# Moving Strassen's sums from GpSimd to VectorE, and the order of two kinds of additions in an attention loop

## The chip, the cores and the metric

The kernel runs on one core of a Trainium2 chip. The metric is the device time of one execution in microseconds (us); smaller is better. The engines are TensorE (PE in the profile; PEld is its weight load), VectorE (DVE), ScalarE (ACT), GpSimd (POOL), and SyncE (SP), whose queue issues most of the DMAs. Each engine executes its instructions in order and waits for the others through semaphores.

## The reference

A batch of 16 images of 256 channels and 32 x 32 pixels (1024 positions) goes through two layers, all in float32. Cut to what matters:

```python
# layer 0: attention over the 1024 positions, 4 heads of 64
qkv = xs @ w_proj + b_proj
attn = softmax(q @ k.T * 64 ** -0.5)
x = (attn @ v) @ w_out + b_out + xs
# layer 1: group norm, attention with 8 heads of 32, then an MLP of 256 -> 1024 -> 256
x = x + attention(group_norm(x), qkv_w, proj_w, proj_b, phys_bias)
h = gelu(mlp_w1 @ group_norm(x) + mlp_b1)
x = x + mlp_w2 @ h + mlp_b2
```

## The kernel before

Channels lie on the 128 partitions in two halves, positions on the free axis[...]. The images follow each other, and one image's stages are mixed with its neighbours' so that TensorE always has matmuls: `attention_a` (layer 0), the MLP's hidden layer of the image before, then `attention_b` (layer 1) with "filler" matmuls in it.

**The second attention** (`attention_b`) runs over 4 items (a position tile and a half of the heads) of 4 units, each unit two key blocks. A unit's `scores` (L502) write eight PSUM tiles, the first two into banks 0 and 1; ScalarE takes their exponentials into four tiles `e_b` of 128 x 1024 (L517, eight buffers). `weigh` multiplies the exponentials of the unit *before* with the values into bank 0 (L553), and the result is added to `res_b`: by ScalarE's copy for an item's first unit (L564), by VectorE for the others (L566). Only after that may the next unit's scores be written to bank 0. VectorE also sums the exponentials into two tiles `es_b` (L532), two additions for the first key block ("block 0") and two for the second. For an item's first unit only the second two exist. The order in the loop is: scores, the additions of block 0, the weighted sums of the unit before with their emptying of bank 0, the additions of block 1.

After a unit, `run` calls `later.tick()` (work put off by so many steps, such as the denominators) and then the unit's filler pieces. In the images 1 to 14 every unit has a filler: q, k and v of the layer 1 heads still missing, q, k and v of the next image's layer 0, and the output products of the previous image's MLP. In image 0 about half the units have none, in the last image (15) some.

**Denominators.** ScalarE copies the sums over keys (L328), SP moves them to a spread layout, VectorE inverts them (L337), SP writes and reads them back through DRAM (`row`, `rd_b`), and VectorE scales `res_b` (L600). GpSimd adds them up in `dsum` and `isum` (L339, L340).

**The MLP.** `hidden` computes 16 tiles `g` of 128 x 512 (matmul L849, Gelu on ScalarE L857). The output layer is a Strassen product: seven products of 128 x 128 blocks (`reduce`, matmul L314 with `m<-g,w2s`) instead of eight. Its right factors are sums and differences of g tiles, made in place by `combine` (L868), four instructions a call: two calls (differences) beside the hidden layer, one each after products 2, 3 and 4. Five of the seven products go to two output blocks: ScalarE copies the bank into a tile `lent` (L911, L914), and two instructions (L929) add or subtract it to the image's tile `x`. The other two go to one block, by one VectorE instruction from the bank (L925). A block that misses nothing more is stored by SP (L931). For all images but the last, L868 and L929 run on GpSimd; for the last, whose MLP stands alone at the end, on VectorE:

```python
add_to = nc.gpsimd if b < B - 1 else nc.vector
```

`nc.…` calls are given in the program's order; a scheduler then orders each engine's instructions by when it expects them to be ready, except those bound by `tc.keep_in_program_order`. The weights' Strassen sums (`sum_quarters`, at the start) stay on GpSimd in both kernels.

Of the kernel before, what the change touches and what calls it, by code (L numbers as in the profile page):

```python
# [11 lines left out]
ALU = mybir.AluOpType  # L12
AX = mybir.AxisListType

P = 128
# [4 lines left out]
TB = 512  # L20
# [215 lines left out]
def first_pass(ctx, tc, x, out, k):  # L236
    nc = tc.nc
    B, C, S = x.shape
    CC, SB, NT = C // P, S // P, S // TB
    HC = k["w1"].shape[2] // P  # L240
    later = Later()
# [25 lines left out]
    def wide(name, n=None):  # L267
        if n is None:
            n = next(m for m in order if m not in kept)
        use(n)  # L270
        return ps_s.tile([P, 2, TB], F32, tag=f"s{n}", name=name)
# [206 lines left out]
    def attention_b(b, qT, kT, v, project):  # L478
        key, D = f"b_{b}", D1
        G = P // D  # L480
# [5 lines left out]
        res, sums = {}, {}  # L486

        def scores(i, kb):
            t, c = items[i]
            es = []  # L490
            for m in range(2):
                if m == 0:
                    one, two = (bank(f"s_{key}_{i}_{kb}_{n}", n) for n in range(2))
                    tiles = [None, wide(f"s_{key}_{i}_{kb}_1")]
                    outs = [one, two, tiles[1][:, 0, :], tiles[1][:, 1, :]]
                else:
                    tiles = [wide(f"s_{key}_{i}_{kb + 1}_{n}") for n in range(2)]
                    outs = [tiles[g // 2][:, g % 2, :] for g in range(G)]
                for g in range(G):
                    for h in range(0, P, HALF):  # L500
                        k0 = (kb + m) * P + h
                        nc.tensor.matmul(  # L502
                            outs[g][h : h + HALF, :],
                            kT[g * D : (g + 1) * D, c, k0 : k0 + HALF],
                            qT[g * D : (g + 1) * D, c, t * TB : (t + 1) * TB],
                            start=True,
                            stop=True,
                        )
                for n in range(G // 2):
                    e = work.tile(  # L510
                        [P, 2, TB], F32, tag="e", name=f"e_{key}_{i}_{kb + m}_{n}", bufs=8
                    )
                    for to, s in (
                        [(e, tiles[n])] if tiles[n] is not None
                        else [(e[:, 0, :], one), (e[:, 1, :], two)]
                    ):
                        nc.scalar.activation(to, s, AF.Exp, scale=float(D) ** -0.5)  # L517
                    es.append(e)
            return i, kb, es

        def add(i, kb, es, block):
            if kb == 0 and block == 0:
                sums[i] = [
                    work.tile([P, 2, TB], F32, tag="es", name=f"es_{key}_{i}_{n}", bufs=4)
                    for n in range(G // 2)
                ]
                return
            for n in range(G // 2):  # L530
                d = sums[i][n]
                ins = nc.vector.tensor_add(d, es[n] if kb == 0 else d, es[2 * block + n])  # L532
                if block:
                    tc.keep_in_program_order(ins)


# [72 lines left out]
        pending = None  # L609
        for u in units:  # L610
            now = scores(*u)
            add(*now, 0)
            if not pending:

                yield
                add(*now, 1)
                pending = now
                continue
            weigh(*pending)
            add(*now, 1)  # L620
            pending = now
            yield
        weigh(*pending)
# [217 lines left out]
    def mlp(b, xb, hn):  # L841
        n4 = HC // 2
        gs = {}
        add_to = nc.gpsimd if b < B - 1 else nc.vector

        def hidden(t, hc):
            ps = wide(f"m1_{b}_{t}_{hc}")[:, 0, :]
            for cc in range(CC):
                nc.tensor.matmul(  # L849
                    ps,  # L850
                    k["w1"][:, cc, hc * P : (hc + 1) * P],
                    hn[0][:, cc, t * TB : (t + 1) * TB],
                    start=(cc == 0),
                    stop=(cc == CC - 1),
                )
            g = work.tile([P, TB], F32, tag="g", name=f"g_{b}_{t}_{hc}", bufs=16)
            nc.scalar.activation(g, ps, AF.Gelu, bias=k["m1b"][:, hc : hc + 1])  # L857
            gs[hc // n4, t, hc % n4] = g
            if (t, hc) == (1, n4):
                combine((1, 0), (0, 0), False)  # L860
            if (t, hc) == (1, HC - 1):
                combine((0, 1), (1, 1), False)


        def combine(to, what, plus):
            for i in range(n4):
                d = gs[(*to, i)]
                ins = (add_to.tensor_add if plus else add_to.tensor_sub)(  # L868
                    d, d, gs[(*what, i)]
                )  # L870
                tc.keep_in_program_order(ins)

        products = [
# [7 lines left out]
        ]  # L883
        missing = {(0, 0): 4, (0, 1): 2, (1, 0): 2, (1, 1): 4}
        lent = []

        def reduce(number, right, outs, then):
            ps = wide(f"m2_{b}_{number}")[:, 0, :]  # L890
            for i in range(n4):
                product(
                    ps, k["w2s"][:, number - 1, i], gs[(*right, i)],
                    start=(i == 0), stop=(i == n4 - 1),
                )
            bias, num, add_to = None, 1, nc.vector
            if len(outs) == 1:
                bias = k["m2b2"]

                num = 2 if b == B - 1 and number == 7 else 1  # L900
            elif number in (2, 5):
                bias = k["m2b"]
            co = outs[0][0]
            if len(outs) == 2:


                if not lent:
                    lent.append(act.tile([P, 4, TB], F32, tag="v0", name=f"lent_{b}"))
                m = lent[0][:, number % 4]
                if bias is not None:  # L910
                    nc.scalar.activation(m, ps, AF.Identity, bias=bias[:, co : co + 1])  # L911
                    bias = None
                else:
                    nc.scalar.copy(m, ps)  # L914
                ps = m
                if b < B - 1:
                    add_to = nc.gpsimd
            for co, t, plus in outs:
                missing[co, t] -= 1
                n = TB // num  # L920
                for u in range(num):
                    sl = slice(t * TB + u * n, t * TB + (u + 1) * n)
                    y, p = xb[:, co, sl], ps[:, u * n : (u + 1) * n]
                    if bias is not None:
                        nc.vector.scalar_tensor_tensor(  # L925
                            y, p, bias[:, co : co + 1], y, ALU.add, ALU.add
                        )
                    else:
                        (add_to.tensor_add if plus else add_to.tensor_sub)(y, y, p)  # L929
                    if not missing[co, t]:  # L930
                        nc.sync.dma_start(out[b, co * P : (co + 1) * P, sl], y)  # L931
            if then:
                combine(*then, True)

        return (
            [lambda t=t, hc=hc: hidden(t, hc) for t in range(NT) for hc in range(HC)],
            [lambda what=what: reduce(*what) for what in products],
        )

# [29 lines left out]
    ps, n = bank("bqk", 0), brow.shape[0]  # L969
# [29 lines left out]
    for b in range(B):  # L999
        if b + 1 < B:  # L1000
# [5 lines left out]
                lambda st, b=b, xn=xn: group_norm(  # L1006
                    f"g{b}", xs[b], st, k["g1w"], k["g1b"], "res", xn, 3
                ),
# [9 lines left out]
        n = len(qk) // CC  # L1018
# [10 lines left out]
        now, end = outputs, []  # L1029
        if b == 0:  # L1030
            first = []
        if b == B - 1:

            now, end = outputs[:3], outputs[3:]
        if not first:
# [3 lines left out]
            now = []  # L1039
# [8 lines left out]
        for m, pieces in enumerate(rest):  # L1048
# [5 lines left out]
                lambda st, b=b, hn=hn: group_norm(  # L1054
                    f"h{b}", xs[b], st, k["g2w"], k["g2b"], "q1", hn,
                    3 if b + 1 < B else 1,
                ),
# [311 lines left out]
```

## Time and profile before

| | |
|---|---|
| median of 3 runs | 3763.86 us (3762.9 to 3764.13) |
| the profiled execution, its own time | 3763.81 us |
| its span, first to last instruction | 3762.0 us |
| mean granted TensorE clock | 0.998 |
| VectorE busy | 2563.5 us, 2700 instructions |
| ScalarE busy | 2085.8 us |
| GpSimd busy | 904.7 us, 701 instructions |

A row of the costliest groups gives: source line, engine, operation, tile written <- tiles read (buffer numbers left out), shapes, count | busy us, mean ns of one | idle time of the engine just before, and who ended it. TensorE's float32 matmul is recorded as two instructions. A timeline row gives the start in us from the span's start, the length, then engine, line, operation and count of merged instructions, and in brackets the idle time before. Busy time of TensorE is modelled at its ends, so idle time is the more telling column.

### The profile page before, as it was taken

Reading aid. Unit: us, or ns where it says so; the run is one execution under the profiler, and the core shown is the slowest. Engines: PE = TensorE matmul, PEld = TensorE weight load, DVE = VectorE, ACT = ScalarE, POOL = GpSimd, SP = SyncE. Lnnn points to the kernel's source line nnn. Section 1 sums busy time; section 2 is a strip of 40 time slices with the busy share of each in tenths; the row PEclk is TensorE's granted clock in tenths of the full one; section 3 lists DMA queues with packets and bytes.
Section 4 is the critical chain, followed back from the end, with each engine's and each line's share of the span. In section 5 each row is a group of like instructions: output and inputs, shape, how many; then the busy total and the mean of one; then the engine's idle time right before and its main releaser. Section 6 shows DMA issues by size and latency. Waiting matters only on the chain.

```text
span 3762.0 us, 79474 instructions
## 1 busy us (share of the span) xinstructions
PE 3699.7 (98%) x34349; PEld 1327.1 (35%) x34349; DVE 2563.5 (68%) x2700; ACT 2085.8 (55%) x2704; POOL 904.7 (24%) x701
## 2 busy tenths in 40 slices
PE   9999999999999999999999999999999999999998
PEld 4333342333423334333333333333333333333423
DVE  4675758667586675867758677586775867758585
ACT  4655546555464554646556465554655546555462
POOL 1002314032140321404114041141401414023121
PEclk9999999999999999999999999999999999999999
DMA  2000100100000000000100101000010100100000
GB/s 85 13 13 10 33 13 13 36 4 33 13 19 30 7 30 13 19 29 7 35 7 19 30 11 32 7 28 20 13 30 7 35 14 13 30 7 24 13 13 21
DMA packets 63395, 77.80 MB, mean 21 GB/s; under 512 B 35038, under 2 KB 37854, under 8 KB 63038
## 3 DMA queue, kind: packets, MB, share of 16 engines
q1 hardware_dynamic: 60892, 71.85, 6.4%
q8 instruction: 271, 4.44, 0.5%
q10 hardware_dynamic: 1746, 0.40, 0.1%
q14 instruction: 86, 0.70, 0.1%
q0 software_dynamic: 400, 0.41, 0.1%
HBM read 54.28 MB, written 17.56 MB: 19 GB/s over the span
## 4 chain that ended last, share of the span: by engine, by line
PE 85%; issue 7%; DVE 5%; DMA 2%; ACT 1%; SPq 0%; ACTq 0%; POOL 0%; DVEq 0%
PE m L849 12%; PE s_a L368 12%; PE acc_a L389 11%; PE s_b L502 11%; PE acc_b L553 9%; PE m L314 6%; PE qk_b L314 6%; PE qk_a L314 4%; PE v_a L314 3%; PE v_b L314 3%; PE o L314 3%; PE j L314 3%; DVE es_b L532 3%; PE den_b L575 1%; DMA rd_b<-row_b 1%
## 5 line engine op out<-in xcount | busy, mean ns | idle before, releaser
L532 DVE TENSOR_TENSOR es_b<-es_b,e_b 128x1024 f32<-128x1024 f32 x768 | 1100.7, 1480 | 249.5 <-ACT e_b L517 249.4
L517 ACT ACTIVATE e_b<-s_b 128x1024 f32<-128x1024 f32 (+1 forms) x1280 | 982.6, 865 | 200.5 <-PE s_b L502 200.5
L376 ACT ACTIVATE e_a<-s_a 128x1024 f32<-128x1024 f32 x512 | 521.0, 1024 | 360.1 <-PE s_a L368 348.4
L502 PE MATMUL s_b<-q,k 32*64 32x512 f32 x8192 | 530.1, 604 | 47.9 <-DVE res_b L566 47.0
L368 PE MATMUL s_a<-q,k 64*64 64x512 f32 x4096 | 532.6, 593 | 1.1
L389 PE MATMUL acc_a<-e_a,v 64*64 64x512 f32 x4096 | 528.5, 589 | 0.0
L401 DVE TENSOR_TENSOR es_a<-es_a,e_a 128x1024 f32<-128x1024 f32 x384 | 469.2, 1222 | 78.0 <-ACT e_a L376 62.3
L868 POOL TENSOR_TENSOR g<-g,g 128x512 f32<-128x512 f32 x300 | 514.1, 1738 | 20.8 <-ACT g L857 20.8
L553 PE MATMUL acc_b<-e_b,v 128*32 128x512 f32 x4096 | 493.1, 599 | 0.0
L849 PE MATMUL m<-gn_h,w 128*128 128x512 f32 x1024 | 452.8, 596 | 0.0
L314 PE MATMUL m<-g,w2s 128*32 128x512 f32 (+1 forms) x3320 | 405.9, 593 | 0.0
L857 ACT ACTIVATE g<-m,m1b 128x512 f32<-128x512 f32 x256 | 176.0, 687 | 343.4 <-PE m L849 343.4
L339 POOL TENSOR_TENSOR dsum<-dsum,sp_b 128x16 f32<-128x16 f32 x63 | 45.0, 715 | 1150.5 <-DMA sp_b<-rd_b 1150.5
L929 POOL TENSOR_TENSOR x<-x,lent 128x512 f32<-128x512 f32 x150 | 268.7, 1811 | 152.6 <-ACT lent L914 96.0
L502 PEld LDWEIGHTS s_b<-q,k 32*64 32x64 f32 x8192 | 164.7, 131 | 381.3 <-issue 166.3
L849 PEld LDWEIGHTS m<-gn_h,w 128*128 128x128 f32 x1024 | 191.0, 190 | 235.9 <-issue 235.7
L389 PEld LDWEIGHTS acc_a<-e_a,v 64*64 64x64 f32 x4096 | 161.9, 133 | 277.6 <-issue 235.6
L368 PEld LDWEIGHTS s_a<-q,k 64*64 64x64 f32 x4096 | 152.6, 133 | 278.1 <-issue 207.9
L314 PE MATMUL qk_a<-x,wp 128*32 128x512 f32 (+1 forms) x1856 | 240.1, 592 | 0.4 <-ACT k L746 0.4
L553 PEld LDWEIGHTS acc_b<-e_b,v 128*32 128x32 f32 x4096 | 108.6, 109 | 359.8 <-ACT e_b L517 196.3
L314 PE MATMUL qk_b<-gn_g,wq 128*32 128x512 f32 (+1 forms) x1280 | 234.0, 592 | 0.0
L314 PEld LDWEIGHTS m<-g,w2s 128*32 128x32 f32 (+1 forms) x3320 | 123.2, 112 | 262.2 <-issue 242.3
(133 smaller groups left out, 2616.8 us busy)
## 6 DMA issues: line engine op xcount, KB each, us to landing
d_a<-row_a SPq DMA_DIRECT2D x64, 256.0 KB
rd_b<-row_b SPq DMA_DIRECT2D x252, 64.0 KB
out_dram<-x SPq DMA_DIRECT2D x63, 256.0 KB
x<-in_x_dram SPq DMA_DIRECT2D x30, 512.0 KB
x<-in_x_dram SPq DMA_DIRECT2D x4, 256.0 KB
w<-in_L_conv_mlp_w_dram SPq DMA_DIRECT2D x1, 1024.0 KB
w2s<-in_L_conv_mlp_w_dram SPq DMA_DIRECT2D x4, 256.0 KB
sp_b<-rd_b SPq DMA_DIRECT2D x63, 8.0 KB
```

The source lines that it names most:

```text
L314: nc.tensor.matmul(o[sl], w[:, sl], r, **flags)
L368: nc.tensor.matmul(s[h : h + HALF, g, :], kT[g * D : (g + 1) * D, c, kb * P + h : kb * P + h + HALF], qT[g * D : (g + 1) * D, c, t * TB : ...
L376: nc.scalar.activation(e, s, AF.Exp, scale=float(D) ** -0.5)
L389: nc.tensor.matmul(accs[i][h][g * D : (g + 1) * D, :], v[h * HALF : (h + 1) * HALF, kb, c * 2 + g], e[h * HALF : (h + 1) * HALF, g, :], st ...
L401: nc.vector.tensor_add(sums[i], held[i] if kb == 1 else sums[i], e)
L502: nc.tensor.matmul(outs[g][h : h + HALF, :], kT[g * D : (g + 1) * D, c, k0 : k0 + HALF], qT[g * D : (g + 1) * D, c, t * TB : (t + 1) * TB] ...
L517: nc.scalar.activation(to, s, AF.Exp, scale=float(D) ** -0.5)
L532: ins = nc.vector.tensor_add(d, es[n] if kb == 0 else d, es[2 * block + n])
L553: nc.tensor.matmul(acc[g * D : (g + 1) * D, :], v[:, kb + m, c * G + g], es[2 * m + g // 2][:, g % 2, :], start=(m == 0), stop=(m == 1),)
L849: nc.tensor.matmul(ps, k["w1"][:, cc, hc * P : (hc + 1) * P], hn[0][:, cc, t * TB : (t + 1) * TB], start=(cc == 0), stop=(cc == CC - 1),)
L868: ins = (add_to.tensor_add if plus else add_to.tensor_sub)(d, d, gs[(*what, i)])
L929: (add_to.tensor_add if plus else add_to.tensor_sub)(y, y, p)
```

## The change

Three things. First, `combine`'s sums and the sums of products into x run on VectorE for every image. Second, they come at other times: `hidden` makes each difference as soon as its second factor is there (one tile at a time, for the first position tile too, instead of four at a time), and a product's sums into x with the `combine` behind it are put off by one step (`later.after(1, add_up)`), to the tick after the next unit's own instructions; no longer bound to the program's order, they may be moved by the scheduler. In the last image's MLP `add_up` still runs at once. Third, in `attention_b` only the first addition of exponentials stands ahead of the weighted sums' emptying of bank 0, and three behind it, instead of two and two.

```diff
-        def add(i, kb, es, block):
-            if kb == 0 and block == 0:
+        def add(i, kb, es, which):
+            if kb == 0 and 0 in which:
                 sums[i] = [
...
-                return
-            for n in range(G // 2):
-                d = sums[i][n]
-                ins = nc.vector.tensor_add(d, es[n] if kb == 0 else d, es[2 * block + n])
-                if block:
+            for n in which:
+                if kb == 0 and n < G // 2:
+                    continue
+                d = sums[i][n % 2]
+                ins = nc.vector.tensor_add(d, es[n % 2] if kb == 0 else d, es[n])
+                if n:
                     tc.keep_in_program_order(ins)
...
         for u in units:
             now = scores(*u)
-            add(*now, 0)
+            add(*now, (0,))
             if not pending:
                 yield
-                add(*now, 1)
+                add(*now, (1, 2, 3))
                 pending = now
                 continue
             weigh(*pending)
-            add(*now, 1)
+            add(*now, (1, 2, 3))
...
-        add_to = nc.gpsimd if b < B - 1 else nc.vector
...
-            if (t, hc) == (1, n4):
-                combine((1, 0), (0, 0), False)
-            if (t, hc) == (1, HC - 1):
-                combine((0, 1), (1, 1), False)
+            if hc >= n4:
+                combine(*(((0, 1), (1, 1)) if t else ((1, 0), (0, 0))), False, hc - n4)
 
-        def combine(to, what, plus):
-            for i in range(n4):
+        def combine(to, what, plus, only=None):
+            for i in range(n4) if only is None else (only,):
                 d = gs[(*to, i)]
-                ins = (add_to.tensor_add if plus else add_to.tensor_sub)(
+                (nc.vector.tensor_add if plus else nc.vector.tensor_sub)(
                     d, d, gs[(*what, i)]
                 )
-                tc.keep_in_program_order(ins)
...
-                if b < B - 1:
-                    add_to = nc.gpsimd
-            for co, t, plus in outs:
...
-                        (add_to.tensor_add if plus else add_to.tensor_sub)(y, y, p)
...
-            if then:
-                combine(*then, True)
+            def add_up():
+                for co, t, plus in outs:
...
+                            (nc.vector.tensor_add if plus else nc.vector.tensor_sub)(y, y, p)
+                        if not missing[co, t]:
+                            nc.sync.dma_start(out[b, co * P : (co + 1) * P, sl], y)
+                if then:
+                    combine(*then, True)
+
+            if len(outs) == 2 and b < B - 1:
+                later.after(1, add_up)
+            else:
+                add_up()
```

More of the change, by code (lines that the diff above doesn't have):

```diff
@@ L895, in reduce @@
                 )
-            bias, num, add_to = None, 1, nc.vector
+            bias, num = None, 1
             if len(outs) == 1:
@@ L915, in reduce @@
                 ps = m
-                if b < B - 1:
-                    add_to = nc.gpsimd
-            for co, t, plus in outs:
[L919 to L931, printed above, removed]
-            if then:
-                combine(*then, True)
+            def add_up():
+                for co, t, plus in outs:
+                    missing[co, t] -= 1
+                    n = TB // num
+                    for u in range(num):
+                        sl = slice(t * TB + u * n, t * TB + (u + 1) * n)
+                        y, p = xb[:, co, sl], ps[:, u * n : (u + 1) * n]
+                        if bias is not None:
+                            nc.vector.scalar_tensor_tensor(
+                                y, p, bias[:, co : co + 1], y, ALU.add, ALU.add
+                            )
+                        else:
[6 more added lines that the diff above has]
+                later.after(1, add_up)
+            else:
+                add_up()
         return (
```

## The prediction

> **What bounds the kernel now.** I read the page's busy shares first, then its costliest groups, then TensorE's waits, then the timeline of one image on TensorE and VectorE, then the granted clock near the end.
>
> The page: engine shares, and the groups that the change touches.
> ```profile
> PE 3699.7 (98%) x34349; PEld 1327.1 (35%) x34349; DVE 2563.5 (68%) x2700; ACT 2085.8 (55%) x2704; POOL 904.7 (24%) x701
> ...
> L532 DVE TENSOR_TENSOR es_b<-es_b,e_b 128x1024 f32<-128x1024 f32 x768 | 1100.7, 1480 | 249.5 <-ACT e_b L517 249.4
> ...
> L502 PE MATMUL s_b<-q,k 32*64 32x512 f32 x8192 | 530.1, 604 | 47.9 <-DVE res_b L566 47.0
> ...
> L868 POOL TENSOR_TENSOR g<-g,g 128x512 f32<-128x512 f32 x300 | 514.1, 1738 | 20.8 <-ACT g L857 20.8
> ...
> L929 POOL TENSOR_TENSOR x<-x,lent 128x512 f32<-128x512 f32 x150 | 268.7, 1811 | 152.6 <-ACT lent L914 96.0
> ```
> TensorE is busy for 98% of the span, and of the idle rest one line owns nearly all: scores (L502) that wait until VectorE has emptied bank 0 (L566). TensorE's waits, one cause a row (total us, times, longest):
> ```profile
> PE s_b L502 <- DVE res_b L566: 47.0, 48, 3.1
> PE gm_h L314 <- DVE mean_c_h L689: 3.4, 1, 3.4
> ```
> TensorE's timeline in the second attention of one middle image shows where:
> ```profile
> 1299.70 1.98 PE L502 MATMUL s_b<-q,k 32*64 32x512 f32 x32 [0.75 <-DVE res_b L566]
> ...
> 1307.62 1.98 PE L502 MATMUL s_b<-q,k 32*64 32x512 f32 x32 [0.65 <-DVE res_b L566]
> ...
> 1315.67 1.97 PE L502 MATMUL s_b<-q,k 32*64 32x512 f32 x32
> ...
> 1322.86 1.97 PE L502 MATMUL s_b<-q,k 32*64 32x512 f32 x32
> ...
> 1330.05 1.97 PE L502 MATMUL s_b<-q,k 32*64 32x512 f32 x32
> ...
> 1338.70 1.98 PE L502 MATMUL s_b<-q,k 32*64 32x512 f32 x32 [1.38 <-DVE res_b L566]
> ```
> A unit (scores, weighted sums of the unit before, a filler) takes 7.19 us when nothing waits (1315.67 to 1322.86 to 1330.05). Three stalls of 0.75, 0.65 and 1.38 us come at the same place in every middle image, 232.15 us apart (1067.56 and 1299.70 for the first of them). Why VectorE is late is in its own timeline, four additions without and with GpSimd at work (L868, L929):
> ```profile
> 1117.30 4.63 DVE L532 TENSOR_TENSOR es_b<-es_b,e_b 128x1024 f32<-128x1024 f32 x4 [3.85 <-ACT e_b L517]
> ...
> 1286.74 8.92 DVE L532 TENSOR_TENSOR es_b<-es_b,e_b 128x1024 f32<-128x1024 f32 x4 [3.44 <-ACT e_b L517]
> ...
> 1298.97 0.67 DVE L566 TENSOR_TENSOR res_b<-res_b,acc_b 128x512 f32<-128x512 f32 x1
> ```
> In the last image some units have no other matmuls to fill them, and the stalls (3.07 and 2.49 us) are long enough to cost clock as well, as the stretches behind them show (columns: window, us, busy PE, PEld, DVE, ACT, POOL, then PEclk):
> ```profile
> 3644.00:3648.00 4.00, 3.67 (x34) 0.92 (x35) 2.54 (x3) 1.66 (x3) 0.00 (x0) 0.50 0.01 2
> ...
> 3667.00:3671.00 4.00, 4.00 (x36) 1.06 (x39) 4.00 (x3) 2.13 (x4) 4.00 (x3) 0.57 0.00 0
> ```
>
> [...] L532 takes 1.22 us at the median and up to 2.31; GpSimd's L868 1.26 at least and up to 2.28. [...] VectorE's own rows of L868 (last image) have 687. [...] here bank 0 serves the weighted sum and then the next scores, and the gap recurs 48 times.
>
> **The change, part by part.** Back to back on VectorE, three sums of 512 take 1.89 us (at 3736.35) and four of 1024 take 4.63 (above): 0.69 + 2 x 0.60 and 1.22 + 3 x 1.14, so I count **0.60 and 1.14 us** each.
>
> *Removed from GpSimd:* 300 sums of hidden factors (L868) and 150 sums into x (L929), 30 in each of 15 images: 783 us of busy time, none of it on the chain by itself. GpSimd keeps the small dsum, isum and rstd instructions; none of them waits behind a sum any more.
>
> *Added to VectorE:* 450 x 0.60 = 270 us. Returned by the end of the contention: L532 896 x (1.43 - 1.14) = 260 us (1282.1 us over 896, both rows by shape), the scaling L600 39 (77.3 - 64 x 0.60), gn_g L722 43 (73.3 against 30.7 for gn_h), three tiny steps L712 to L716 47 (54.4 - 48 x 0.16). That is 389, so VectorE's total **falls** by about 119 us to some 2445.
>
> *Where the 30 sums land.* Eight subtractions stand beside the hidden layer (L857), each when its Gelu is out; VectorE has slack there (9.57 us idle ahead of the first L767), and in the built program's order of VectorE's instructions gn_g stands before the later four. The two that stand ahead of x<-o end at about 1221.2, that one starts at 1221.5 now: nothing, unless the Gelu slips by 0.3 us. The other 22 (12 sums, 10 into x) come in bunches of six or two. In the built order they stand mostly after one unit's four additions, where VectorE would wait for the next exponentials. From 1284 to 1343 VectorE then works 26 x 1.14 + 8 x 0.60 + 22 x 0.60 + 0.5 = 48 us of 56 (now 52.9 of 59).
>
> *The weighted sum's emptying, one addition earlier.* Replaying the middle image by hand: the bunch of the first product runs 1283.3 to 1287.1, the unit's four additions end at 1291.7 (now 1295.7). The next emptying starts as soon as its matmuls end (1295.5) and frees bank 0 at 1296.3; TensorE wants it at 1299.0. The second: free 1303.5, wanted 1306.2. The third: free 1333.3, wanted 1335.9. The tightest unit between (scores of the third item's last pair) still has 1.9 us, so all three stalls go. What is saved is the pitch: the three stalled units take 8.01 (1291.69 to 1299.70), 7.92 and 8.65 us (1330.05 to 1338.70), over 7.19 by 0.82 + 0.73 + 1.46 = 3.01 us an image. 14 x 3.01 = **42.1 us**. Nothing on TensorE's path is late next: ScalarE works 59 of the 90 us from 1253 to 1343.
>
> *First image.* Its units are unfilled and the four stalls sum to 2.5 us (0.70, 0.43, 0.92, 0.43). There the emptying follows its matmuls at once and the next scores want the bank at once, so VectorE's 18.5 us of work in a 21.5 us item decides. **1.7 us**.
>
> *Last image.* Stalls of 5.56 us, plus clock: (1 - 0.50) x 4 + (1 - 0.74) x 4 (3648 to 3652) + (1 - 0.57) x 4 = 4.8. My replay frees the bank at 3641.3 instead of 3644.3, and the second within about 0.1 us of need; a bunch of six sums ahead of one emptying costs 0.4. **9.8 us**.
>
> *Tail.* gm_h waits 3.38 us, the last projection 1.04, and 3695 to 3700 ran at clock 0.71 (1.45 lost). In the built order two matmuls of product 6 now stand ahead of gm_h (1.8 us) and the scaling L600 is not held (1.70 to 0.69), but four sums of g stand among the means and gv_h to gn_h is less covered. Between 0 and 5; I take **3.5**.
>
> *DMAs.* SP's order is as before. Its stores of x (L931) wait for the sums into x, and behind them in SP's queue wait the denominators' transfers; the sums of product 3 end near 1310.6 instead of 1312.1, those of product 4 at 1323.4 instead of 1327.5, so nothing is held longer. The reciprocal comes earlier too, and its transfer has over 6 us, as in the first image (180.75 to 186.81 without a wait). Price nothing.
>
> Sum: 42.1 + 1.7 + 9.8 + 3.5 = 57.1. The profiled execution took 3763.81 us (span 3762.0, 1.8 around it), the median of the runs is 3763.86, so 3763.8 - 57.1 = **3707**. Floor: TensorE's idle column sums to 55.3, of which 1.9 at the start stays; 53.4 + 48 x 0.08 of lost overlap (0.82 against the stall's 0.75) + 6.2 of clock = 63.4: 3700.
>
> **Rivals.** (A) *Only the filled units gain.* In the unfilled units of the first and last image VectorE has no slack, and its waits there only shift: 42.1 alone, 3722. For it: the 18.5 of 21.5 us. Against: in the last image the contention (L600 1.75 instead of 0.68, additions of 2.3) is what makes VectorE late. (B) *Sums block the bank.* VectorE runs in order; if the bunch of six (3.7 us, with a wait for ScalarE's copy to lent) falls between the matmuls' end and the emptying, the bank is free 0.7 + 3.7 = 4.4 us after those matmuls, where 3.6 us of fill cover it: 0.8 + 0.07 lost. Five such products make 4.4 us an image against 3.0 saved, and the ends gain nothing: 3764 + 14 x 1.4 = 3783, **slower**. It decides once the bank is free later than 4.2 us after its matmuls in all five. For it: in the built order one bunch (product 3) does stand ahead of an emptying. Against: that unit has a 3.6 us fill and a den, and my replay leaves it 2.9 us. (C) *The wait moves on.* TensorE's stall is taken over by exponentials (L517) or by e's eight buffers at the same length: 3764, no change. Against: ScalarE idles 200.5 us ahead of L517 for TensorE, not the reverse.
>
> **How the numbers follow.** As forecast 0.79 (own range 3701 to 3715, the tail's 0 to 5 and 3 us of the ends), A 0.13 (3717 to 3728), C 0.03, B 0.05. The range 3701 to 3727 holds the first and most of A. 0.2% (7.5 us) is about what a measurement of this kernel can tell from no change: faster 0.92, within it 0.03, slower 0.05.
>
> **What would show it.** Right: L502 waiting for the emptying under 3 us in all; three rows of 1.38, 0.65, 0.75 gone and an image period of 229.1 us; L532 near 1220 ns; VectorE near 2445 us; GpSimd x251; no stretch at clock 0.5 near the end. Wrong: L532 still near 1480; a stall in the middle images owned by the emptying, g, lent or e_b; gn_g later than qk_b wants it.

## The result and the profile after

The changed kernel takes **3707.52 us** (median of 4 runs, 3707.03 to 3709.13) against 3763.54 us of the kernel before beside it, a ratio of 0.9852 with the interval 0.9835 to 0.9869: 56.0 us faster. Its profiled execution took 3707.96 us, span 3706.2, against 3763.81 and 3762.0 before.

The page of the changed kernel, busy shares and groups (L532 is now L533, L566 is L567, L868 is L866, L767 is L768):

```profile
PE 3685.2 (99%) x34349; PEld 1319.4 (36%) x34349; DVE 2498.0 (67%) x3150; ACT 2084.0 (56%) x2704; POOL 102.9 (3%) x251
...
L533 DVE TENSOR_TENSOR es_b<-es_b,e_b 128x1024 f32<-128x1024 f32 x768 | 899.5, 1219 | 217.2 <-ACT e_b L517 217.1
...
L502 PE MATMUL s_b<-q,k 32*64 32x512 f32 x8192 | 527.2, 601 | 9.8 <-DVE v L768 7.1
...
L866 DVE TENSOR_TENSOR g<-g,g 128x512 f32<-128x512 f32 x320 | 209.3, 686 | 147.7 <-ACT g L857 147.4
```

VectorE has 450 instructions more and is busy 65 us less: an addition of exponentials takes 1219 ns in the mean, not 1480. TensorE's waits are down from 55.3 to 13.9 us in all; the first rows:

```profile
PE s_b L502 <- DVE v L768: 7.1, 16, 1.2
PE s_b L502 <- DVE res_b L567: 1.6, 2, 0.9
```

The emptying of bank 0 has gone from 47.0 to 1.6 us. A row that was not among the seven of before leads now: scores that wait for VectorE's emptying of `v`. In TensorE's timeline of the same middle image the rows at 1287.45, 1294.64 and 1324.26 are the three that stalled before. None has a wait, and each comes 7.19 us after the unit ahead of it:

```profile
1273.07 1.97 PE L502 MATMUL s_b<-q,k 32*64 32x512 f32 x32
...
1280.26 1.97 PE L502 MATMUL s_b<-q,k 32*64 32x512 f32 x32
...
1287.45 1.97 PE L502 MATMUL s_b<-q,k 32*64 32x512 f32 x32
...
1294.64 1.97 PE L502 MATMUL s_b<-q,k 32*64 32x512 f32 x32
...
1317.07 1.97 PE L502 MATMUL s_b<-q,k 32*64 32x512 f32 x32
...
1324.26 1.97 PE L502 MATMUL s_b<-q,k 32*64 32x512 f32 x32
```

Four additions take 4.62 us, where two stretches of before had 4.63 and 8.92. They follow the moved sums without a gap (two sums into x stand between the rows shown):

```profile
1271.79 2.51 DVE L866 TENSOR_TENSOR g<-g,g 128x512 f32<-128x512 f32 x4
...
1275.43 4.62 DVE L533 TENSOR_TENSOR es_b<-es_b,e_b 128x1024 f32<-128x1024 f32 x4
```

The new wait, 0.33 us in every middle image, is seen a little earlier in the same image. First TensorE, then VectorE:

```profile
1257.24 1.11 PE L502 MATMUL s_b<-q,k 32*64 32x512 f32 x16
1258.68 1.12 PE L502 MATMUL s_b<-q,k 32*64 32x512 f32 x16 [0.33 <-DVE v L768]
```

```profile
1252.28 1.23 DVE L533 TENSOR_TENSOR es_b<-es_b,e_b 128x1024 f32<-128x1024 f32 x1 [1.97 <-ACT e_b L517]
1253.93 0.69 DVE L567 TENSOR_TENSOR res_b<-res_b,acc_b 128x512 f32<-128x512 f32 x1 [0.43 <-PE acc_b L554]
1254.54 3.49 DVE L533 TENSOR_TENSOR es_b<-es_b,e_b 128x1024 f32<-128x1024 f32 x3
1257.94 0.69 DVE L768 TENSOR_TENSOR v<-v_b,eones 128x512 f32<-128x512 f32 x1
```

VectorE waits 0.43 us for the matmuls before it can empty bank 0, so the emptying was not late at all; then three additions, not two, stand ahead of the emptying of `v`, whose PSUM tile the next scores want.

Where the 55.8 us between the spans come from, read by setting TensorE's instructions of both kernels side by side and parting the images at the first scores of each second attention: first image -0.1, fourteen middle periods 42.0 (232.15 to 229.14 us each, one of them to 229.35), last image with its tail 13.9.

### The profile page after: what moved, and what is told of

Read it like the earlier page. It is cut to its first block, busy times and chain, and to the rows that moved or that the text cites. A ratio compares the mean times of both kernels' runs of the same rounds, so it can differ in the third digit from the quotient of the medians.

```text
span 3706.2 us, 79254 instructions
## 1 busy us (share of the span) xinstructions
PE 3685.2 (99%) x34349; PEld 1319.4 (36%) x34349; DVE 2498.0 (67%) x3150; ACT 2084.0 (56%) x2704; POOL 102.9 (3%) x251
## 4 chain that ended last, share of the span: by engine, by line
PE 94%; DVE 3%; issue 2%; ACT 1%; DMA 1%; ACTq 0%; SPq 0%; POOL 0%; DVEq 0%
PE s_b L502 12%; PE acc_b L554 12%; PE s_a L368 12%; PE m L849 12%; PE acc_a L389 11%; PE m L314 10%; PE qk_a L314 6%; PE qk_b L314 5%; PE o L314 3%; PE v_a L314 3%; PE j L314 3%; PE v_b L314 2%; PE den_b L576 1%; DVE es_b L533 1%; PE den_a L420 1%
## 5 line engine op out<-in xcount | busy, mean ns | idle before, releaser
L533 DVE TENSOR_TENSOR es_b<-es_b,e_b 128x1024 f32<-128x1024 f32 x768 | 899.5, 1219 | 217.2 <-ACT e_b L517 217.1
L866 DVE TENSOR_TENSOR g<-g,g 128x512 f32<-128x512 f32 x320 | 209.3, 686 | 147.7 <-ACT g L857 147.4
L567 DVE TENSOR_TENSOR res_b<-res_b,acc_b 128x512 f32<-128x512 f32 x192 | 131.8, 687 | 143.7 <-PE acc_b L554 143.7
L768 DVE TENSOR_TENSOR v<-v_b,eones 128x512 f32<-128x512 f32 x64 | 44.1, 689 | 166.0 <-PE v_b L314 166.0
```

The costliest lines, as they stand in the source:

```text
L533: ins = nc.vector.tensor_add(d, es[n % 2] if kb == 0 else d, es[n])
L866: (nc.vector.tensor_add if plus else nc.vector.tensor_sub)(d, d, gs[(*what, i)])
```

## Experiments

**The two halves of the change, each alone.** Order only: the kernel before with one addition ahead of the emptying and three behind; all sums stay on GpSimd.

```diff
-            add(*now, 0)
+            add(*now, (0,))
             ...
-            add(*now, 1)
+            add(*now, (1, 2, 3))
```

> The kernel before, with the change of order alone: one addition of exponentials ahead of the emptying of bank 0 and three behind it; all Strassen sums stay on GpSimd. My theory: [...] in a middle image one addition less ahead frees the bank 1.2 to 2.3 us earlier, so the stalls of 0.75 and 0.65 us go and the one of 1.38 shrinks to about 0.2; v's emptying costs 0.45 as in the kernel after. That is some 2.3 us an image, 3727 to 3735 in all, with L532 still near 1430 to 1480 ns and the last image's slow clock still there. Rival (the sums' engine is all that counts): 3760 to 3764.

Measured: 3788.77 us, ratio 1.0066 (1.0051 to 1.0081), 25.0 us slower than before. The expectation had it 29 to 37 us faster. TensorE's waits in this kernel, largest first:

```profile
PE den_b L576 <- DVE es_b L533: 25.1, 28, 0.9
PE s_b L502 <- DVE res_b L567: 9.3, 27, 2.0
PE s_b L502 <- DVE v L768: 7.1, 16, 1.2
```

The emptying did come in time, from 47.0 us down to 9.3. But what was moved behind it became late for someone else. The denominators' matmuls read the finished sums of exponentials, and twice an image they wait for the last addition (TensorE's timeline):

```profile
1318.55 0.62 PE L576 MATMUL den_b<-es_b,eones 128*32 128x512 f32 x2 [0.90 <-DVE es_b L533]
...
1350.33 0.62 PE L576 MATMUL den_b<-es_b,eones 128*32 128x512 f32 x2 [0.89 <-DVE es_b L533]
```

Per middle image the instructions set side by side show 2.38 us gained at the three old stalls (one of them leaves 0.32), 0.52 lost to `v`, and 3.4 lost at and behind the denominators' two waits of 0.9 (some 1.9 and 1.5). The period is 1.55 us longer, 14 x 1.55 = 21.7 of the 25.0. An addition beside GpSimd still takes up to 2.31 us, and three of them in a row are too many.

Engine only: the changed kernel with the old two-and-two order. It keeps the new times of the sums, so it is parts one and two of the change together.

```diff
-            add(*now, (0,))
+            add(*now, 0)
             ...
-            add(*now, (1, 2, 3))
+            add(*now, 1)
```

> The kernel after, with the old order of two additions ahead of the emptying of bank 0 and two behind it; the sums stay on VectorE. My theory: [...] VectorE has done both additions when the weighted sums end, so none of the three stalls returns in the middle images, and the wait of L502 for v (0.33 us an image, 0.45 in pitch, over 1 us in the first and last image) goes: 14 x 0.45 + 2.1 gained, some 2 lost again in the unfilled units of the first and last image: 3700 to 3704, a little faster than after. Rival (the order is what removed the stalls): the three stalls come back in part, 3725 to 3745.

Measured: 3699.36 us, ratio 0.9829 (0.9815 to 0.9842), 64.4 us faster than before, 8.2 faster than the full change and a little below the expected range. The wait for `v` is not in its list; the first row is

```profile
PE s_b L502 <- DVE res_b L566: 4.1, 6, 1.1
```

So moving the sums does all of the work and some more, and the new order costs. With the two together:

| | two and two | one and three |
|---|---|---|
| sums on GpSimd | 3763.5 (before) | 3788.8 |
| sums on VectorE | 3699.4 | 3707.5 (after) |

**The order only where it costs nothing.** The changed kernel, with two and two in the first item of each image (where `v` is emptied) and one and three in the rest.

```diff
+        def ahead(i):
+            return (0, 1) if i == 0 else (0,)
+
+        def behind(i):
+            return (2, 3) if i == 0 else (1, 2, 3)
             ...
-            add(*now, (0,))
+            add(*now, ahead(now[0]))
```

> The kernel after, but in each image's first item (where v is made) two additions stand ahead of the emptying and two behind it; elsewhere one and three. My theory: v's emptying on VectorE stood one addition later in after, and that alone made the new wait; with it gone 14 x 0.45 + 2 x 1.06 = 8.4 us are gained: 3698 to 3701. Rival (the wait for v comes from the sums on VectorE or from elsewhere): 3706 to 3709.

Measured: **3697.98 us**, ratio 0.9825 (0.9812 to 0.9839), 9.5 us faster than the full change and the fastest kernel here; from engine-only, 1.4 us away, its interval doesn't part it. The period is 228.62 us, 0.52 less than after, as in engine-only. VectorE at the same place of a middle image: two additions ahead of `v`, and no wait of the scores behind it.

```profile
1251.68 2.35 DVE L539 TENSOR_TENSOR es_b<-es_b,e_b 128x1024 f32<-128x1024 f32 x2
1253.95 0.68 DVE L774 TENSOR_TENSOR v<-v_b,eones 128x512 f32<-128x512 f32 x1
```

That settles the wait for `v`: it belongs to the first item's third addition. The gain over the full change is 14 x 0.52 = 7.3, and 1.1 each from the same wait in the first and last image (1.2 us long there).

**A step behind, or at once.**

```diff
-            if len(outs) == 2 and b < B - 1:
-                later.after(1, add_up)
-            else:
-                add_up()
+            add_up()
```

> The kernel after, with the sums of a product issued at once instead of a step behind. In the built program every engine's order is the same as in after but for some 20 VectorE instructions near the end, since the scheduler places the sums by when they are ready. My theory: 3706 to 3710, and identical stalls in the middle images. Rival (the step behind is what keeps ScalarE's copy from holding VectorE): over 3715.

Measured: 3707.87 us, ratio 0.9854 (0.9839 to 0.9869): no difference from the full change. Putting the sums off by a step does nothing here: in the traces only 22 of VectorE's 3150 instructions stand at another place in its order, since the scheduler places the sums in nearly the same order either way.

**Contention alone, with VectorE's order kept.** The changed kernel, with 22 GpSimd additions for each of 15 images (330 in all) that read `g` and `lent` in SBUF and write to a tile that nobody reads any more.

```diff
+                if len(outs) == 2 and b < B - 1:
+                    for _ in range(2):
+                        nc.gpsimd.tensor_add(ps, ps, ps)
+                    for i in range(n4) if then else ():
+                        o = gs[(*then[1], i)]
+                        nc.gpsimd.tensor_add(ps, o, o)
```

> The kernel after, in which GpSimd also adds two tiles of 128x512 into a tile that is no longer needed, behind every bunch of VectorE's sums: 22 additions in each of 15 second attentions, 330 in all, read by nobody. The order of every other engine's instructions is that of after. My theory [...]: L533 goes from 1219 to about 1350 to 1450 ns in the mean, VectorE cannot keep up in the units with products, and stalls of 2 to 10 us an image return: 3740 to 3850. Rival (the sums mattered by their place in a queue or by what waits for them[...]): 3706 to 3710.

Measured: 3785.86 us, ratio 1.0063 (1.0046 to 1.008), 78 us slower than after. Its group of additions, and the wait that leads TensorE's list:

```profile
L533 DVE TENSOR_TENSOR es_b<-es_b,e_b 128x1024 f32<-128x1024 f32 x768 | 1047.7, 1410 | 116.2 <-ACT e_b L517 116.1
```

```profile
PE s_b L502 <- DVE res_b L567: 55.0, 46, 2.1
```

The additions went from 1219 to 1410 ns, and the wait for the emptying came back from 1.6 to 55.0 us, three stalls in a middle image (0.91, 0.63 and 2.10 us) where before had three, now with one and three in force. Two rows of VectorE's timeline there, three additions as one row and one scaling:

```profile
1102.35 5.42 DVE L533 TENSOR_TENSOR es_b<-es_b,e_b 128x1024 f32<-128x1024 f32 x3
1107.69 1.52 DVE L601 TENSOR_TENSOR res_b<-res_b,rd_b 128x512 f32<-128x512 f32 x1
```

Three additions take 5.42 instead of 3.49 us and the scaling 1.52 instead of 0.68. GpSimd's additions are the cause: in the traces TensorE, ScalarE and VectorE compute the same instructions in the same order as in the full change, and no wait is put down to the added ones (ScalarE has 71 semaphore instructions more, without a wait for GpSimd). What the two engines contend for, the runs do not show.

**The last image alone.** The kernel before, with the sums of the one image whose MLP runs beside the last image's attention on VectorE.

```diff
-        add_to = nc.gpsimd if b < B - 1 else nc.vector
+        add_to = nc.gpsimd if b < B - 2 else nc.vector
         ...
-                if b < B - 1:
+                if b < B - 2:
                     add_to = nc.gpsimd
```

> The kernel before, in which only the sums of image 14's MLP, which run inside the last image, are on VectorE; the old order, issued at once. My theory: [...] 12 to 16 us gained, 3748 to 3752, with no stretch below a clock of 0.9 near the end. Rival (the last image's stalls are owed to units without filler, whatever the engine): under 4 us gained, 3760 to 3764.

Measured: 3750.47 us, ratio 0.9966 (0.9954 to 0.9979), 12.8 us faster than before: nearly all of the 13.9 that the full change gains there, from 30 of the 450 sums. The stretch at clock 0.50 behind the first stall is gone (the stall is 0.43 us now), and gm_h no longer waits. The second stall stays, 2.55 us long, and 3.41 us at clock 0.50 begin inside it, so the expectation missed there:

```profile
PE s_b L502 <- DVE res_b L566: 45.0, 49, 2.6
```

GpSimd has no sum to do there. In VectorE's timeline six sums (3655.72 to 3659.34) stand ahead of two additions and the emptying of bank 0, for which the scores wait until 3662.34. This is what the prediction's rival B feared, in one unit:

```profile
3655.72 1.29 DVE L929 TENSOR_TENSOR x<-x,lent 128x512 f32<-128x512 f32 x2 [1.37 <-ACT lent L914]
3656.94 2.49 DVE L868 TENSOR_TENSOR g<-g,g 128x512 f32<-128x512 f32 x4
3659.34 2.35 DVE L532 TENSOR_TENSOR es_b<-es_b,e_b 128x1024 f32<-128x1024 f32 x2
3661.61 0.68 DVE L566 TENSOR_TENSOR res_b<-res_b,acc_b 128x512 f32<-128x512 f32 x1
```

**No sums at all.** The changed kernel leaves out the 450 sums; all else stays.

```diff
             for i in range(n4) if only is None else (only,):
                 d = gs[(*to, i)]
+                if b < B - 1:
+                    continue
```

> The kernel after with the 450 sums of the first 15 images' MLP left out altogether (factors and products are not combined there); the stores of x stay. My theory: VectorE's added 270 us of work lie wholly beside TensorE's, and the wait for v stays since it comes from the order of the exponentials' additions: 3702 to 3708. Rival [...]: below 3700.

Measured: 3706.85 us, ratio 0.9851 (0.9834 to 0.9867), 0.7 us from the full change. VectorE is busy 2223.0 us instead of 2498.0, 275 less, and TensorE's first wait stays:

```profile
PE s_b L502 <- DVE v L768: 7.0, 16, 1.2
```

So the 275 us of added work on VectorE cost nothing measurable, and the wait for `v` has nothing to do with the sums.

**The order taken further.** The changed kernel with no addition ahead of the emptying and four behind.

```diff
-            add(*now, (0,))
             if not pending:
                 ...
-                add(*now, (1, 2, 3))
+                add(*now, (0, 1, 2, 3))
```

> The kernel after with no addition of exponentials ahead of the emptying of bank 0 and all four behind it. My theory: the emptying was not late any more with one or two ahead, so nothing is gained there, while v's emptying comes one addition (1.14 us) later still: its stall grows from 0.33 to about 1.5 us in each of 16 images, 3720 to 3728. Rival (the earlier the bank is emptied, the better): 3700 to 3707.

Measured: 3738.03 us, ratio 0.9934 (0.9917 to 0.9951), 30.5 us slower than after, more than was expected. The list and the last image's timeline show why:

```profile
PE s_b L502 <- DVE v L767: 26.3, 16, 2.4
```

```profile
3572.24 1.98 PE L502 MATMUL s_b<-q,k 32*64 32x512 f32 x8 [2.42 <-DVE v L767]
```

In a middle image the wait grows by one addition, 0.33 to 1.53 us: 14 x 1.20 = 16.8. In the first and in the last image it grows from 1.22 to 2.42 us, and there it takes clock with it. The windows behind it, first and last image (the number behind POOL's busy time and count is PEclk):

```profile
144.00:148.00 4.00, 4.00 (x24) 0.79 (x20) 0.00 (x0) 1.03 (x1) 0.00 (x0) 0.58 0.00 0
...
3574.00:3578.00 4.00, 4.00 (x24) 0.99 (x24) 0.15 (x1) 1.02 (x1) 0.00 (x0) 0.50 0.00 0
```

The matmuls behind the wait take twice as long for a while (in the last image the weighted sums just behind it 3.64 us, those of the unit before 1.92), which costs 3.0 us in the last image by TensorE's instructions side by side; the first image loses 5.3 in all and the last 6.7. What the expectation left out is this clock, and a second wait in the last image (1.8 us for bank 0).

## Why the prediction was right, and where not

The forecast, 3707, is 0.5 us from the measured median, within the range and on the right side. That GpSimd's sums hold VectorE up, as it had it, is what the runs show: an addition of exponentials took 1480 ns in the mean and up to 2.31 us before, 1219 and 1.24 at most after. Its terms are less good than its sum, which came so near because misses of either sign cancel: that part is luck.

- **Middle images, 42.1 forecast, 42.0 measured.** The three stalls went as worked out, 0.82 + 0.73 + 1.46. "Nothing on TensorE's path is late next" failed: the emptying of `v` was, 0.33 us of idle time, 0.52 of pitch. I followed bank 0 and the denominators' transfers when the third addition was moved, but not the other emptyings in VectorE's queue. Its loss was offset by luck: the third item's denominators waited for additions stretched by GpSimd before (4.6 us over 14 waits of the weight loads), and without contention they don't, some 0.5 gained an image. That gain is in no idle column of TensorE, so the floor of 3700 was not one: engine-only measured 3699.4 and the run with two and two in the first item 3698.0.
- **What does it.** The step "the weighted sum's emptying, one addition earlier" gave both edits one sum. Engine-only shows that the gain does not need the order: with two and two the bank comes free in time as well. That it is the end of the contention, and not the sums' new times, is shown by two runs: GpSimd's additions alone, with everything else in place, cost 78 us, and leaving the sums out changes 0.7. A bank more for the weighted sum was not tried. The order alone costs 25.0 us beside GpSimd, and 8.2 without it.
- **First image, 1.7 forecast, -0.1 measured.** Three units gained 0.62 us each by the order. The wait for `v` took 1.14, the last denominators' matmuls 0.37, and the stretch from a wait ahead of the first attention's output matmuls on some 0.5. All but the last are the order's: engine-only has none of them.
- **Last image and tail, 9.8 + 3.5 forecast, 8.6 + 5.3 measured** (parted ahead of the last projection). The stalls of 3.07 and 2.49 us are both gone, and no window near the end is below 1.00 until the matmuls run out; 1.1 us is lost again to `v`. The tail gained more than its range of 0 to 5. A unit that did not wait before has a wait of 0.65 us now, and 0.51 for ScalarE's copy behind it: six sums (VectorE, 3578.94 to 3582.55) stand just ahead of its emptying. In the run without the sums the first is gone, and waits for ScalarE's copy are 0.2 at most. It is the bunch of six that the prediction priced at 0.4. The last-only run puts 12.8 us of the gain on one image's sums.

```profile
3580.75 1.89 DVE L866 TENSOR_TENSOR g<-g,g 128x512 f32<-128x512 f32 x3
3582.55 0.68 DVE L567 TENSOR_TENSOR res_b<-res_b,acc_b 128x512 f32<-128x512 f32 x1
```

- **VectorE's total, 2445 forecast, 2498 measured.** Of the 389 us to be returned, the rows show 355: additions 1282.1 - 1050.2 = 231.9 instead of 260, the scaling 33.5, gn_g 42.6, the tiny steps 46.6. Added were 275 (no-sums) instead of 270. The mis-sized term is the additions': from the busy time of one in the rows, 1.43 us, I took off the pitch of additions back to back, 1.14, though the rows count even an undisturbed one as 1.17 (1050.2/896). These rows leave some 14 us of the difference open. It cost the time nothing, since VectorE has that slack.
- **DMAs and subtractions at nothing:** no wait for either is on TensorE's list, as argued.
- **Rivals.** A, that only the filled units gain, fell for the last image and held for the first. B, a bunch of sums that blocks the bank, happened in one unit of the last image and nowhere in the middle ones: taking all bunches away gains 0.7 us. C, a wait that moves on at the same length, did not come with both edits; order-only shows such a move, to the denominators instead of the exponentials.

## What to carry to other kernels

Where an engine is late, ask first why its instructions are long: here moving 783 us of GpSimd work onto VectorE made VectorE less busy (2563.5 to 2498.0 us) and freed TensorE (waits of 55.3 to 13.9 us), since an addition of exponentials took up to 2.31 us with GpSimd's sums beside it and 1.24 at most without. VectorE kept its order when it was late, too: in the run with GpSimd's additions, 78 us longer, it computed the same instructions in the same order. So before an instruction is put ahead in such a queue, list every later consumer of what falls behind it (here `v`'s PSUM tile and the denominators), not only the wait one wants rid of. A change of two edits deserves a run of each alone: here one gained 64 us, and the other gave 8 of them back.

## What was not expected of the hardware

- Work that nobody needs cost as much here as real work: 330 GpSimd additions whose results are unused cost 78 us, 0.24 us each, though TensorE and VectorE had no instruction more. The 450 real ones, in the same order of additions, cost 81 (3788.8 against 3707.5).
- The same wait of TensorE did or did not cost clock. In the run with GpSimd's additions a stall of 2.10 us stands at the same place of all fourteen middle images. Behind six of them, every second one from the third on, the clock was 0.50 for 3.41 us; behind the other eight it stayed at 1.00. Two of the fourteen, and a stall of 2.12 us in the last image:

```profile
1112.00:1116.00 4.00, 4.00 (x56) 1.20 (x56) 4.00 (x5) 3.03 (x5) 0.09 (x1) 1.00 0.02 4
...
1346.00:1350.00 4.00, 4.00 (x32) 0.71 (x20) 3.66 (x5) 3.81 (x5) 0.20 (x1) 0.57 0.00 0
...
3667.00:3671.00 4.00, 4.00 (x38) 0.87 (x26) 4.00 (x3) 2.75 (x4) 1.90 (x1) 0.57 0.02 6
```

The six falls begin 467.63 us apart, which is 137 x 3.413, and in each trace here all falls begin whole multiples of 3.413 us apart. In these traces the cost goes with how a wait lies in a grid of such steps. The stall that ends at 1344.85 lies in one step for 2.06 us and was followed by a fall; the one that ends at 1111.85 is parted into 0.94 and 1.16 and was not. Ahead of the last matmuls the traces have 17 falls, and TensorE had idled 1.79 to 3.07 us in the step before 16 of them. Two cases do not fit: a fall behind 1.22 us (order-only, last image) and none behind 1.88 us (the first of the fourteen stalls). So no step had to be idle throughout for the clock to fall: 1.79 us of 3.41 were enough in these traces. What sets the grid and the falls is not shown, and no run here was made to test it.
